# Seven wide steps of a node stage on GpSimd instead of VectorE, in a two-layer graph kernel

## The chip, the cores and the metric

The kernel runs on one core of a Trainium2 chip. A core has a matrix engine (TensorE, PE in the profile), a vector engine (VectorE, DVE), an activation engine (ScalarE, ACT), a general engine (GpSimd, POOL) and a queue engine for transfers (SyncE, SP). Each works through its own queue of instructions in order, and they meet through semaphores. The metric is the device time of one execution in microseconds; the profile's span runs from the first to the last instruction.

## The reference

3327 nodes with 64 features, a dense adjacency matrix of zeros and ones. Two layers, each of the form x = x + layer(relu(layernorm(x))).

```python
# layer 0: hyperbolic attention over neighbours (c = 1 / r^2)
x_t = logmap0(h, c)
left, right = x_t @ w_att[:64, 0], x_t @ w_att[64:, 0]
adj_att = sigmoid(left[:, None] + right[None, :] + b_att[0]) * adj
x_local = logmap(h[:, None, :], h[None, :, :], c)
support = einsum('ij,ijd->id', adj_att, x_local)
out0 = proj(expmap(h, support, c), c)
# layer 1: of each row's neighbours the last 100 count, halved with each step back
rank = cumsum(adj != 0, axis=1); deg = rank[:, -1:]
k = minimum(deg, 100); pos = rank - (deg - k)
w = (adj != 0) * where(pos > 0, 0.5 ** (k - pos), 0)
out1 = w @ (h1 @ weight) + bias
```

Layer 0 needs a value for every pair of nodes. Layer 1 needs, for every pair, how many neighbours lie behind it in its row.

## The kernel before

Nodes are padded to 26 blocks of 128. The pairs are walked in four strips of target nodes, 8, 8, 6 and 4 blocks wide (1024, 1024, 768 and 512 columns), and in each strip over the 26 source blocks from the last to the first. A round is one source block of a strip, except that a round of the last strip takes two, so that all but the third strip's rounds are 1024 columns wide: 91 rounds in all. The main loop runs over the rounds and writes out by hand the order in which PE, DVE and ACT get their instructions.

In a round, PE computes products into a PSUM tile `pq` (lines 680 and 681), counts neighbours into a PSUM tile `pc` from a 0/1 mask (634, 635), and sums finished weights times features into `po` (693). ACT applies two gelus in place to `pq` (873, 874) and a tanh into a tile `sg` (663). DVE does `pair_one`, (sg + 1) * adjacency, both in SBUF (668); `edges`, the mask of a later round from its adjacency tile (623); and `pair_two`, (pq + const) * sg, with `pq` in PSUM (673). The count in `pc` is read out into small integers by `read`, on ACT (652) or on DVE (654, 656); a table `ON_ACT` says for each strip what share of the rounds goes to ACT (1/2, 5/8, 3/4, 1/2).

When a strip ends, its sums `po` are copied out (`strip_out`, 1175 on DVE and 1177 on ACT), transposed by PE (1187, `turn`), copied again (1197, 1199, `per_node`), and then go through `post`, the node stage: norms, the exponential map, the addition to x, layer norm and split of the result into two half-precision parts `s2`, which layer 1 multiplies. For the first three strips this stage is hidden under the next strip's rounds: `post` is a generator, and `advance` takes some of its steps in each round, up to a number of portions. Small steps on 8 or 6 values per partition are collected and given to GpSimd (all at line 1062). Wide steps, on 64 values of each node (512 or 384 per partition), are DVE's: 1080, 1082, 1084, 1140 to 1151, 1156, 1162 and 1167. ACT's wide steps (1154, 1165) wait for a place after the gelus. The last strip's stage is not hidden under rounds; it runs in layer 1, on DVE, among the decoding of weights (1336, 1339, 1340). The bias of layer 1 is added to x by GpSimd (1352). At the end the last four blocks are multiplied (1237), copied (1378 to 1382), multiplied by the weight (1390), added to x (1392) and stored.

The order around a round's stage:

```python
        pair_one(n)
        if two: read(m, js(m)[0])
        if EARLY <= m + 1 < R: edges(m + 1)
        if fresh: count(m, js(m)[-1])
        if n + 1 < R: sigmoids(n + 1)
        if fresh: read(m, js(m)[-1])
        if 4 <= n < R - 1: products(n + 1)
        if ended: strip_out(k - 1)
        if hi - lo > 1: advance(PORTIONS[k])
        pair_two(n)
        advance(PORTIONS[k])
```

Of the kernel before, what the change touches and what calls it, by code (L numbers as in the profile page):

```python
# [12 lines left out]
F32 = mybir.dt.float32  # L13
# [5 lines left out]
AF = mybir.ActivationFunctionType  # L19
ALU = mybir.AluOpType  # L20
# [3 lines left out]
P = 128  # L24
N = 3327
NB = 26
NP = NB * P
D = 64
# [5 lines left out]
AHEAD, LOADS = 1, 4  # L34
EARLY = 3
SGB, ADB = 5, 5
ON_ACT = ((1, 2), (5, 8), (3, 4), (1, 2))


PORTIONS, LAST = (2, 4, 4, 8), 8  # L40
BIG, LATER, ACT = 4, 99, 100
ROUND = (3.5, 3.5, 2.8, 1.9)

LEAD = 7
# [405 lines left out]
def fast(ctx, tc, x, adj_t, r, w_att, b_att, weight, bias, out, flag):  # L450
# [76 lines left out]
    def wide(t, n):  # L527
        return t[:, :, None].to_broadcast([P, n, D])
# [91 lines left out]
    def edges(n):  # L620
        mask_of[n] = mask = work.tile([P, FMAX], BF16, name="mask", bufs=3)
        args = mask[:, : span(n)], ad_of[n][:, : span(n)]
        V.tensor_scalar(*args, 0.0, None, op0=ALU.not_equal)  # L623
# [17 lines left out]
    def read(n, j, on_act=None):  # L641
        k, lo, hi = rounds[n]
        S = strips[k]
        kept = behind(j)[:, S.i0 : S.i0 + S.F]
        num, den = ON_ACT[k]
        i = NB - 1 - j
        of = S.pc[:, : S.F]
        if j in JD:
            kept = by_parity(weight_of[:, j - JD.start])[:, :, S.i0 // 2 : (S.i0 + S.F) // 2]
            of = of.rearrange("p (k r) -> p r k", r=2)  # L650
        if on_act or (on_act is None and i * num // den != (i + 1) * num // den):
            A.activation(kept, of, AF.Relu, scale=128.0 if j in JD else 1.0)  # L652
        elif j in JD:
            V.tensor_scalar(kept, of, 0.0, 128.0, op0=ALU.max, op1=ALU.mult)
        else:
            V.tensor_scalar(kept, S.pc[:, : S.F], 0.0, None, op0=ALU.max)  # L656

    def sigmoids(n):

        S = strips[rounds[n][0]]  # L660
        sg_of[n] = sg = work.tile([P, FMAX], F32, name="sg", bufs=SGB)
        for j in js(n):
# [205 lines left out]
    A.copy(nz[:, high, 0], zf[:, high])  # L868
    V.tensor_copy(nu[:, high, :D], zf[:, high])

    def gelus(n):
        pq = pq_of[n][:, : span(n)]
        A.activation(pq, pq, AF.Gelu, scale=-WG / QS)  # L873
        A.activation(pq, pq, AF.Gelu, scale=WH)  # L874

    def logits(bs, plr=None):

# [132 lines left out]
    def post(agg, k):  # L1010
# [36 lines left out]
        def root(y, v):  # L1047
# [7 lines left out]
            else:  # L1055
                W.scalar_tensor_tensor(rt, v, -0.5, rt, op0=ALU.mult, op1=ALU.mult)
                W.scalar_tensor_tensor(y, rt, 1.5, y, op0=ALU.add, op1=ALU.mult)

        def after(time):

            for do, args, kwargs in asked_of_w:
                do(*args, **kwargs)  # L1062
                if not hidden:
                    yield from [LATER] * 2 if kwargs.get("op") == ALU.pow else [1]
            asked_of_w.clear()
            if hidden:
                yield from [LATER] * math.ceil(time / ROUND[k + 1])

        def both(t):
            return t[:, None, :].to_broadcast([P, 2, nb])  # L1070
# [6 lines left out]
        u, w = tile_of("u", nb, D), tile_of("w", nb, D)  # L1077

        A.activation(u, v, AF.Square)
        V.tensor_mul(w, hs, v)  # L1080
        yield BIG
        V.tensor_reduce(dots[:, 1], w, AX.X, ALU.add)  # L1082
        yield BIG
        V.tensor_reduce(dots[:, 2], u, AX.X, ALU.add)
# [14 lines left out]
        root(rn, t0)  # L1099
        mul(t0, t0, rn)  # L1100
        mul(t0, t0, sk[:, bs])
        yield from after(8.5)
        yield ACT
        A.activation(k_, t0, AF.Tanh)
        yield 0
# [34 lines left out]
        V.tensor_mul(w, hs, wide(of_end[:, 0], nb))  # L1140
        yield BIG
        V.tensor_mul(u, v, wide(of_end[:, 1], nb))
        yield BIG
        V.tensor_add(xs, xs, w)
        yield BIG
        V.tensor_add(xs, xs, u)
        yield BIG

        V.tensor_reduce(t0, xs, AX.X, ALU.add)
        yield BIG  # L1150
        V.scalar_tensor_tensor(w, wide(t0, nb), -1.0 / D, xs, op0=ALU.mult, op1=ALU.add)  # L1151
        yield BIG
        yield ACT
        A.activation(u, w, AF.Square)
        yield 0
# [8 lines left out]
        yield ACT  # L1164
        A.copy(s2[:, bs, 0], w)
        yield 0
        V.tensor_sub(s2[:, bs, 1], w, s2[:, bs, 0])
        yield BIG

    def strip_out(k):  # L1170
        S = strips[k]
        S.ot = work.tile([P, FMAX], F32, name="sg", bufs=SGB)[: D + 1]
        for po, (f0, f1) in zip(S.po, S.hv):
            if f0 == 0:
                V.tensor_copy(S.ot[:, f0:f1], po[: D + 1, : f1 - f0])
            else:
                A.copy(S.ot[:, f0:f1], po[: D + 1, : f1 - f0])
# [23 lines left out]

    class Stage:
        def __init__(self, portions):
            self.portions, self.asked = portions, False

    def advance(portions):
        for stage in stages:
            while portions > 0 and not stage.asked:
                portion = next(stage.portions, LATER)
                stage.asked = portion == ACT  # L1210
                if portion >= LATER:
                    break
                portions -= portion

    def asked_of_act():
        for stage in stages:
            if stage.asked:
                next(stage.portions)
                stage.asked = False

    def finish():
        for stage in stages:
# [21 lines left out]
    for n in range(2, R):  # L1244
# [13 lines left out]
            pa = turn(k - 1)  # L1258
        if n >= 4 and (apart or not turned):
            total(n - 2)  # L1260
        gelus(n)
        asked_of_act()
        if turned and not apart:
            finish()
            stages.append(Stage(per_node(k - 1, pa)))
# [2 lines left out]
            read(m, js(m)[0])  # L1268
        if EARLY <= m + 1 < R:
            edges(m + 1)  # L1270
        if n == 2:
            for j in js(2):
                read(2, j, True)
# [3 lines left out]
            total(1)  # L1277
        if fresh:
            count(m, js(m)[-1])
        if n + 1 < R:  # L1280
            sigmoids(n + 1)
        if fresh:
            read(m, js(m)[-1])
        if 4 <= n < R - 1:
            products(n + 1)
        if ended:
            strip_out(k - 1)
        if hi - lo > 1:
            advance(PORTIONS[k])
        if turned and apart:  # L1290
# [29 lines left out]
        add(j, behind(j), n)  # L1320
    pa = turn(len(STRIPS) - 1)
    pairs.close()
    with tc.tile_pool(name="l1", bufs=2, reuse_waits="tile") as l1, tc.manual_schedule(engines=IN_ORDER):
        decoded = 0

# [21 lines left out]
        for n, j in beside:  # L1347
            add(j, behind(j), n)

        def bias(b0, nb):  # L1350
            xb = x_sb[:, b0 : b0 + nb]
            G.tensor_add(xb, xb, bias_b[:, None, :].to_broadcast([P, nb, D]))  # L1352

        for i, j in enumerate(order):
            for jn in every[: i + 1 + LEAD]:
                if jn not in weights:
                    weights[jn] = decode(jn)
            asked_of_act()
            advance(LAST)
            for n in range(len(chunks)):  # L1360
                if j not in JD or n > 4:
                    add(j, weights[j], n)
            if i % 4 == 3 and i < STRIPS[-2][0]:
                bias(i - 3, 4)
# [93 lines left out]
```

## Time and profile before

| | us |
|---|---|
| three runs | 404.16, 401.86, 404.40 (median 404.16) |
| the profiled execution | 404.32 |
| its span | 402.6 |
| mean granted clock of PE | 0.99 |

The busy time of an engine is what it spent in instructions; a row of a group gives the line, the engine, the operation, output and inputs, the shape, the count, then busy us and mean ns of one, then idle time of the engine just before and what ended it. A row of the timeline gives the start in us, the duration, and in brackets the wait before it and the releaser.

GpSimd's 240 instructions before are almost all small: those of line 1062 on 8 values per partition take from 0.20 us to 2.7 us.

### The profile page before, as it was taken

Reading aid. Unit: us, or ns where it says so; the run is one execution under the profiler, and the core shown is the slowest. Engines: PE = TensorE matmul, PEld = TensorE weight load, DVE = VectorE, ACT = ScalarE, POOL = GpSimd, SP = SyncE. Lnnn points to the kernel's source line nnn. Section 1 sums busy time; section 2 is a strip of 40 time slices with the busy share of each in tenths; the row PEclk is TensorE's granted clock in tenths of the full one; section 3 lists DMA queues with packets and bytes.
Section 4 is the critical chain, followed back from the end, with each engine's and each line's share of the span. In section 5 each row is a group of like instructions: output and inputs, shape, how many; then the busy total and the mean of one; then the engine's idle time right before and its main releaser. Section 6 shows DMA issues by size and latency. Waiting matters only on the chain.

```text
span 402.6 us, 4731 instructions
## 1 busy us (share of the span) xinstructions
PE 355.0 (88%) x1460; PEld 151.9 (38%) x1460; DVE 367.3 (91%) x563; ACT 355.3 (88%) x407; POOL 118.1 (29%) x240
## 2 busy tenths in 40 slices
PE   0087999999999999999999899999979899999992
PEld 0063333333333333333333444444433233344462
DVE  4989999999999989999999999899999999898941
ACT  3589999999999999999999999999998999869510
POOL 8145200000000053870052052850240767241200
PEclk9999999999999899999999999999999999999997
DMA  7314555454548435553445545544563440000012
GB/s 202 150 42 133 171 157 158 128 165 138 163 139 237 148 106 156 156 157 109 153 116 148 149 120 157 131 134 128 152 188 117 111 152 0 0 2 1 2 42 52
DMA packets 23298, 48.99 MB, mean 122 GB/s; under 512 B 8789, under 2 KB 9245, under 8 KB 23265
## 3 DMA queue, kind: packets, MB, share of 16 engines
q1 hardware_dynamic: 20993, 47.66, 40.3%
q10 hardware_dynamic: 1808, 0.46, 0.6%
q0 software_dynamic: 464, 0.49, 0.5%
q8 instruction: 13, 0.21, 0.2%
q14 instruction: 20, 0.16, 0.1%
HBM read 46.40 MB, written 0.87 MB: 117 GB/s over the span
## 4 chain that ended last, share of the span: by engine, by line
DVE 32%; ACT 32%; PE 19%; issue 12%; DMA 1%; POOL 1%; POOLq 0%; DVEq 0%; ACTq 0%
ACT sg L663 11%; ACT pq L873 9%; DVE sg L673 8%; DVE sg L668 7%; PE po L693 7%; ACT behind_lo L652 3%; ACT pq L874 3%; PE pc L635 2%; PE pc L634 2%; PE pq L680 2%; PE pq L681 2%; ACT weight_of L652 2%; DVE behind_hi L656 2%; DVE mask L623 1%; ACT behind_hi L652 1%
## 5 line engine op out<-in xcount | busy, mean ns | idle before, releaser
L693 PE MATMUL po<-sg,hw 128*65 128x512 f32 (+1 forms) x364 | 159.5, 561 | 0.0
L673 DVE SCALAR_TENSOR_TENSOR sg<-pq,sg 128x1024 f32<-128x1024 f32 (+1 forms) x91 | 103.8, 1140 | 4.4 <-ACT pq L874 3.8
L668 DVE SCALAR_TENSOR_TENSOR sg<-sg,ad 128x1024 f32<-128x1024 f32 (+1 forms) x91 | 104.1, 1144 | 0.2
L663 ACT ACTIVATE sg<-left_b,right 128x1024 f32<-128x1024 f32 (+2 forms) x103 | 99.5, 978 | 0.0
L874 ACT ACTIVATE pq<-pq 128x1024 f32<-128x1024 f32 (+1 forms) x91 | 86.2, 947 | 2.9
L873 ACT ACTIVATE pq<-pq 128x1024 f32<-128x1024 f32 (+1 forms) x91 | 87.1, 958 | 1.1 <-PE pq L681 0.9
L693 PEld LDWEIGHTS po<-sg,hw 128*65 128x65 f32 x364 | 49.0, 137 | 67.3 <-issue 53.9
L634 PE MATMUL pc<-mask,ca 128*128 128x512 bf16 (+1 forms) x175 | 64.0, 366 | 10.1 <-ACT behind_hi L652 2.8
L680 PE MATMUL pq<-iu,ju 71*128 71x512 f16 (+1 forms) x182 | 67.5, 371 | 1.6 <-ACT jz L810 1.0
L635 PE MATMUL pc<-mask,cb 128*128 128x512 bf16 (+1 forms) x182 | 65.2, 369 | 1.8 <-ACT behind_lo L652 1.7
L681 PE MATMUL pq<-iz,jz 128*128 128x512 f16 (+1 forms) x182 | 65.9, 369 | 0.0
L623 DVE TENSOR_SCALAR mask<-ad 128x1024 bf16<-128x1024 f32 (+1 forms) x91 | 58.8, 647 | 0.0
L1062 POOL TENSOR_TENSOR dots<-dots,ih 128x8 f32<-128x8 f32 (+1 forms) x3 | 3.1, 1022 | 130.0 <-DVE dots L1082 130.0
L635 PEld LDWEIGHTS <-cb 128*128 128x128 bf16 x182 | 17.8, 98 | 51.8 <-issue 40.3
L634 PEld LDWEIGHTS <-ca 128*128 128x128 bf16 x175 | 17.2, 98 | 29.5 <-issue 17.3
L680 PEld LDWEIGHTS <-ju 71*128 71x128 f16 x182 | 17.9, 99 | 23.1 <-DVE sg L673 5.1
L1237 PEld LDWEIGHTS <-s 128*128 128x128 f16 x182 | 17.7, 98 | 20.2 <-issue 1.5
L681 PEld LDWEIGHTS <-jz 128*128 128x128 f16 x182 | 18.1, 99 | 19.1 <-issue 2.1
L652 ACT ACTIVATE behind_lo<-pc 128x1024 uint8<-128x1024 f32 (+2 forms) x29 | 24.9, 859 | 0.0
L1352 POOL TENSOR_TENSOR x_sb<-x_sb,bias_b 128x256 f32<-128x256 f32 (+1 forms) x6 | 8.6, 1443 | 51.7 <-DVE w L1151 46.0
L652 ACT ACTIVATE behind_hi<-pc 128x1024 uint8<-128x1024 f32 (+2 forms) x25 | 21.8, 871 | 1.2 <-PE pc L635 1.2
L844 PE MATMUL pq<-id,nui 128*71 128x128 f16 x8 | 1.0, 311 | 21.2 <-ACT nzi L818 21.2
(336 smaller groups left out, 396.0 us busy)
## 6 DMA issues: line engine op xcount, KB each, us to landing
ad<-in_adj_t SPq DMA_DIRECT2D x65, 512.0 KB, 3.6
ad<-in_adj_t SPq DMA_DIRECT2D x26, 384.0 KB, 3.1
out<-o SPq DMA_DIRECT2D x6, 128.0 KB, 1.9
left_b<-left_d SPq DMA_DIRECT2D x1, 512.0 KB, 5.0
x_sb<-in_x ACTq DMA_DIRECT2D x1, 416.0 KB, 5.7
x_sb<-in_x SPq DMA_DIRECT2D x1, 416.0 KB
left_b<-left_d SPq DMA_DIRECT2D x1, 384.0 KB
jz<-iz POOLq DMA_DIRECT2D x2, 128.0 KB, 2.6
```

Source lines behind the costliest of these rows:

```text
L623: V.tensor_scalar(*args, 0.0, None, op0=ALU.not_equal)
L634: T.matmul(S.pc[:, f0:f1], ca, S.before[:, f0:f1], start=False, stop=True, skip_group_check=True)
L635: T.matmul(S.pc[:, f0:f1], cb, now[:, f0:f1], start=S.first, stop=True, skip_group_check=True)
L652: A.activation(kept, of, AF.Relu, scale=128.0 if j in JD else 1.0)
L663: A.activation(part(n, sg, j), S.left[:, : S.F], AF.Tanh, bias=right[:, j : j + 1], scale=0.5)
L668: V.scalar_tensor_tensor(sg, sg, 1.0, ad_of.pop(n)[:, :w], op0=ALU.add, op1=ALU.mult)
L673: V.scalar_tensor_tensor(sg, pq_of.pop(n)[:, :w], WD, sg, op0=ALU.add, op1=ALU.mult)
L680: T.matmul(part(n, pq, j, f0, f1), ju[:KB, j, :], S.iu[:, f0:f1], start=True, stop=False)
L681: T.matmul(part(n, pq, j, f0, f1), jz[:, j, :], S.iz[:, f0:f1], start=False, stop=True)
L693: T.matmul(po[: D + 1, : f1 - f0], hw[:, j, :], part(n, sg_of[n], j, f0, f1), start=j == NB - 1, stop=j == 0)
L873: A.activation(pq, pq, AF.Gelu, scale=-WG / QS)
L874: A.activation(pq, pq, AF.Gelu, scale=WH)
```

## The change

Seven wide steps of each hidden stage go from DVE to GpSimd: the product for the first dot, the two products and two additions of the update, the subtraction of the mean (the mean's scaling becomes a small step of its own), and the last subtraction for `s2`. They are given out at a new place in the round, after `edges`, when the last read was ACT's or in the last strip; the four update steps go in two groups of two. Ahead of each step GpSimd copies one column of the newest mask into the step's output, so that the step cannot start before that mask is written. The update's first sum goes to `agg` instead of `x_sb`.

The table `ON_ACT` is gone: reads alternate between ACT and DVE, and the one after a wide step on DVE is ACT's; in the last strip the second read of a round is ACT's. The strip copies come before the tanh and the read. In the last two strips the first tanh of the next round stands between the two gelus. Two bias additions go to DVE near the end. The order of PE's instructions is the same as before.

```diff
-ON_ACT = ((1, 2), (5, 8), (3, 4), (1, 2))
-BIG, LATER, ACT = 4, 99, 100
+BIG, LATER, ACT, POOL = 4, 99, 100, 101
...
     def read(n, j, on_act=None):
+        if hi - lo > 1:
+            on_act = j == lo
...
-        if on_act or (on_act is None and i * num // den != (i + 1) * num // den):
+        if on_act is None:
+            on_act = wide_step[0] or not last_on_act[0]
+            if not wide_step[0]:
+                last_on_act[0] = on_act
+            wide_step[0] = False
+        if on_act:
             A.activation(kept, of, AF.Relu, scale=128.0 if j in JD else 1.0)
...
+    def gelu(n, scale):
+        pq = pq_of[n][:, : span(n)]
+        A.activation(pq, pq, AF.Gelu, scale=scale)
...
+        def on_pool(*steps):
+            if hidden:
+                yield POOL
+                for op, to, *of in steps:
+                    if last_mask[0] is not None:
+                        G.tensor_copy(to[:, 0, :1], last_mask[0][:, :1])
+                    getattr(G, op)(to, *of)
+                yield 0
+            else:
+                for op, *args in steps:
+                    getattr(V, op)(*args)
+                    yield BIG
...
-        V.tensor_mul(w, hs, v)
-        yield BIG
+        if hidden:
+            G.tensor_copy(w[:, 0, :1], last_mask[0][:, :1])
+            G.tensor_mul(w, hs, v)
+            yield LATER
+        else:
+            V.tensor_mul(w, hs, v)
+            yield BIG
...
-        yield from after(8.5)
+        yield from after(7)
...
-        V.tensor_mul(w, hs, wide(of_end[:, 0], nb))
-        yield BIG
-        V.tensor_mul(u, v, wide(of_end[:, 1], nb))
-        yield BIG
-        V.tensor_add(xs, xs, w)
-        yield BIG
-        V.tensor_add(xs, xs, u)
-        yield BIG
+        yield from on_pool(("tensor_mul", w, hs, wide(of_end[:, 0], nb)), ("tensor_mul", u, v, wide(of_end[:, 1], nb)))
+        yield from on_pool(("tensor_add", v, xs, w), ("tensor_add", xs, v, u))
+        if hidden:
+            yield LATER
         V.tensor_reduce(t0, xs, AX.X, ALU.add)
         yield BIG
-        V.scalar_tensor_tensor(w, wide(t0, nb), -1.0 / D, xs, op0=ALU.mult, op1=ALU.add)
-        yield BIG
+        W.tensor_scalar(t0, t0, 1.0 / D, None, op0=ALU.mult)
+        do_asked()
+        yield from on_pool(("tensor_sub", w, xs, wide(t0, nb)))
...
-        V.tensor_sub(s2[:, bs, 1], w, s2[:, bs, 0])
-        yield BIG
+        yield from on_pool(("tensor_sub", s2[:, bs, 1], w, s2[:, bs, 0]))
...
     def advance(portions):
                 portion = next(stage.portions, LATER)
-                stage.asked = portion == ACT
+                wide_step[0] |= portion == BIG
+                stage.asked = portion if portion in (ACT, POOL) else None
...
-        gelus(n)
-        asked_of_act()
+        tanh_first = k > 1 and n + 1 < R
+        gelu(n, -WG / QS)
+        if tanh_first:
+            sigmoids(n + 1, slice(1))
+        gelu(n, WH)
+        list(asked_of(ACT))
...
             edges(m + 1)
+            last_mask[0] = mask_of[m + 1]
+        if last_on_act[0] or k + 1 == len(STRIPS):
+            list(asked_of(POOL))
...
+        if ended:
+            strip_out(k - 1)
         if n + 1 < R:
-            sigmoids(n + 1)
+            sigmoids(n + 1, slice(tanh_first, None))
         if fresh:
             read(m, js(m)[-1])
         if 4 <= n < R - 1:
             products(n + 1)
-        if ended:
-            strip_out(k - 1)
...
         for i, j in enumerate(order):
-            asked_of_act()
+            list(asked_of(ACT))
+            list(asked_of(POOL))
             advance(LAST)
...
-        bias(STRIPS[-2][0], late - STRIPS[-2][0])
-        bias(late, NB - late)
...
             copied(n)
+            if n == 2:
+                bias(STRIPS[-2][0], late - STRIPS[-2][0], V)
+                bias(late, NB - late, V)
```

More of the change, by code (lines that the diff above doesn't have):

```diff
@@ L644, in read @@
         kept = behind(j)[:, S.i0 : S.i0 + S.F]
-        num, den = ON_ACT[k]
-        i = NB - 1 - j
+        if hi - lo > 1:
+            on_act = j == lo
         of = S.pc[:, : S.F]
@@ L656, in read, with sigmoids @@
             V.tensor_scalar(kept, S.pc[:, : S.F], 0.0, None, op0=ALU.max)
-    def sigmoids(n):
+    wide_step, last_on_act, last_mask = [False], [False], [None]
+    def sigmoids(n, of=slice(None)):
         S = strips[rounds[n][0]]
-        sg_of[n] = sg = work.tile([P, FMAX], F32, name="sg", bufs=SGB)
-        for j in js(n):
+        if n not in sg_of:
+            sg_of[n] = work.tile([P, FMAX], F32, name="sg", bufs=SGB)
+        sg = sg_of[n]
+        for j in js(n)[of]:
             A.activation(part(n, sg, j), S.left[:, : S.F], AF.Tanh, bias=right[:, j : j + 1], scale=0.5)
@@ L869, in fast @@
     V.tensor_copy(nu[:, high, :D], zf[:, high])
+    def gelu(n, scale):
+        pq = pq_of[n][:, : span(n)]
+        A.activation(pq, pq, AF.Gelu, scale=scale)
     def gelus(n):
-        pq = pq_of[n][:, : span(n)]
-        A.activation(pq, pq, AF.Gelu, scale=-WG / QS)
-        A.activation(pq, pq, AF.Gelu, scale=WH)
+        gelu(n, -WG / QS)
+        gelu(n, WH)
     def logits(bs, plr=None):
@@ L1057, in root, with do_asked @@
                 W.scalar_tensor_tensor(y, rt, 1.5, y, op0=ALU.add, op1=ALU.mult)
+        def do_asked():
+            for do, args, kwargs in asked_of_w:
+                do(*args, **kwargs)
+            asked_of_w.clear()
         def after(time):
@@ L1203, in __init__ @@
         def __init__(self, portions):
-            self.portions, self.asked = portions, False
+            self.portions, self.asked = portions, None
     def advance(portions):
@@ L1213, in advance, with asked_of @@
                 portions -= portion
-    def asked_of_act():
+    def asked_of(engine):
         for stage in stages:
-            if stage.asked:
+            if stage.asked == engine:
                 next(stage.portions)
-                stage.asked = False
+                stage.asked = None
+                yield engine
     def finish():
@@ L1260, in fast @@
             total(n - 2)
-        gelus(n)
-        asked_of_act()
+        tanh_first = k > 1 and n + 1 < R
+        gelu(n, -WG / QS)
+        if tanh_first:
+            sigmoids(n + 1, slice(1))
+        gelu(n, WH)
+        list(asked_of(ACT))
         if turned and not apart:
@@ L1322, in fast @@
     pairs.close()
+    last_mask[0] = None
     with tc.tile_pool(name="l1", bufs=2, reuse_waits="tile") as l1, tc.manual_schedule(engines=IN_ORDER):
@@ L1348, in fast, with bias @@
             add(j, behind(j), n)
-        def bias(b0, nb):
+        def bias(b0, nb, engine=G):
             xb = x_sb[:, b0 : b0 + nb]
-            G.tensor_add(xb, xb, bias_b[:, None, :].to_broadcast([P, nb, D]))
+            engine.tensor_add(xb, xb, bias_b[:, None, :].to_broadcast([P, nb, D]))
         for i, j in enumerate(order):
```

## The prediction

> **What bounds the kernel now.** I read the busy shares first, then busy time by stretch, then the groups kept apart by shape, then the timeline where engines meet, and last the waits of the tail.
>
> ```profile
> PE 355.0 (88%) x1460; PEld 151.9 (38%) x1460; DVE 367.3 (91%) x563; ACT 355.3 (88%) x407; POOL 118.1 (29%) x240
> ```
>
> Three engines are nearly full and GpSimd (POOL) is idle 71% of the time. An average hides where each binds, so the next view cuts the span where DVE's L673 changes strip: 41.8 to 126.9 us is strip 0, then strips 1, 2 and 3 (columns: length, busy PE, PEld, DVE, ACT, POOL, then clock, DMA share, GB/s).
>
> ```profile
> 126.90:223.10 96.20, 92.33 (x319) 34.95 (x318) 93.00 (x103) 94.21 (x102) 34.23 (x62) 0.98 0.49 142
> 223.10:300.30 77.20, 71.06 (x316) 33.57 (x315) 73.31 (x100) 76.25 (x104) 28.44 (x62) 1.00 0.50 142
> 300.30:350.50 50.20, 46.13 (x160) 17.15 (x159) 49.38 (x65) 48.34 (x65) 23.77 (x52) 1.00 0.28 84
> ```
>
> The stage of strip k runs under the rounds of strip k+1, so these rows are where the change acts. In strip 1 all three engines are within 4 us of full. Strip 2 is ACT's: it lacks 1.0 us, DVE 3.9. Strip 3 is DVE's: it lacks 0.8, ACT 1.9. PE's missing time (3.9, 6.1 and 4.1 us) caps what DVE and ACT relief can win: 14.1 us, since the PE order is the same before and after. Strip 0 is unchanged: its rounds alternate 2.87 and 4.00 us, a mean of 3.44, and PE's own spacing (eight matmuls at 0.215, four at 0.43) is 3.44 as well.
>
> The prices:
>
> ```profile
> L673 DVE SCALAR_TENSOR_TENSOR sg<-pq,sg 128x1024 f32<-128x1024 f32 x65 | 79.1, 1216 | 1.4 <-ACT pq L874 0.8
> L656 DVE TENSOR_SCALAR behind_lo<-pc 128x1024 uint8<-128x1024 f32 x10 | 12.2, 1218 | 0.0
> L656 DVE TENSOR_SCALAR behind_lo<-pc 128x768 uint8<-128x768 f32 x3 | 2.9, 951 | 0.2 <-PE pc L635 0.2
> L1140 DVE TENSOR_TENSOR w<-hw,of_end 128x512 f32<-128x512 f32 x2 | 1.4, 682 | 0.0
> L1140 DVE TENSOR_TENSOR w<-hw,of_end 128x384 f32<-128x384 f32 x1 | 0.5, 549 | 0.0
> ```
>
> Durations of neighbours on DVE overlap by about 0.085 us in the timeline (a 1.22 us instruction starts 1.13 after the one before), so I charge 0.60 for a wide step of 512, 0.47 for 384, 1.14 and 0.87 for a read of 1024 and 768; on ACT 0.92 and 0.72 for such reads.
>
> **The change part by part.**
>
> *Wide steps leave DVE.* Seven per stage: two stages of 512 and one of 384: 14 x 0.60 + 7 x 0.47 = 11.7 us off DVE, 4.2 under strip 1, 4.2 under strip 2, 3.3 under strip 3.
>
> *Reads move to DVE.* By the two instruction orders DVE gains one read in strip 1 and four in strip 2; ACT loses them. DVE +1.1 and +3.5, ACT -0.9 and -2.9. Net on DVE without contention: -3.1, -0.7, -3.3.
>
> *What GpSimd pays and gives back.* It gains 21 wide steps, 19 one-column tie copies and 3 scalings, and loses two bias additions. The nearest row is the bias addition; here it is beside DVE:
>
> ```profile
> 286.50 0.95 DVE L668 SCALAR_TENSOR_TENSOR sg<-sg,ad 128x768 f32<-128x768 f32 x1
> 286.67 2.54 POOL L1352 TENSOR_TENSOR x_sb<-x_sb,bias_b 128x256 f32<-128x256 f32 x2 [18.52 <-DVE w L1151]
> 287.37 0.55 DVE L623 TENSOR_SCALAR mask<-ad 128x768 bf16<-128x768 f32 x1
> 287.84 0.95 DVE L673 SCALAR_TENSOR_TENSOR sg<-pq,sg 128x768 f32<-128x768 f32 x1
> 288.71 1.30 DVE L668 SCALAR_TENSOR_TENSOR sg<-sg,ad 128x768 f32<-128x768 f32 x1
> ```
>
> Two things are to be seen. L668 and the mask ran at full speed while GpSimd had already been issued: GpSimd was kept out until 287.92, then did two 256-wide additions by 289.21, 0.64 each. And the second L668 took 1.30 instead of 0.95: it waited 0.35 for the addition in flight. L673, which takes one operand from PSUM, did not. So a 512-wide step costs about 1.25 us in a clear stretch (an estimate, twice 0.62), a 384 one 0.93; doubling the group's mean of 1.31 per 256 would give 2.6, but that mean contains the waiting. The Trainium skill, "SBUF — State Buffer", section "Who interferes with whom", speaks against the change: a DVE instruction with two SBUF inputs or in a two-port mode and a GpSimd instruction exclude each other for the whole instruction, whoever comes second. Both rows agree with the blocking; they differ in size. By the rule, all 21 steps could land on L668 or the mask: 14 x 1.25 + 7 x 0.93 = 24 us of blocking. By the row the cost is only the overhang, 0.35 us for a pair of 256.
>
> The tie makes a pair start when a mask ends, in a round whose read is DVE's (last strip: any round). From there to the next L668 the clear window is read plus L673: 2.28 us in strip 1, 1.74 in strip 2; in strip 3 L673 alone, 1.14. A pair takes two ties (0.5 with gaps: a copy of 128x8 took 0.19 to 0.21) and two steps: 3.0 us, or 2.4 for 384. Overhang 0.7 a pair in strip 1, 1.25 in strip 2 if the second step has just started (0.4 if DVE gets in first), up to 1.2 in strip 3. I take 0.7, 0.9 and 0.6, two pairs each, and 0.3 a stage for the three single steps, which fit at 1.5 us: 1.7 + 2.1 + 1.5 = 5.3 us on DVE; bounds 1 and 24. DVE then stands at -1.4, +1.4, -1.8.
>
> Behind the ties on GpSimd's queue stand only the stage's own small steps; those who wait are DVE's reductions (L1149, L1082), placed a round later, and ACT's square and cast. A round of 2.8 us or more covers a 3.0 us pair begun at its mask and read after the next round's L673. If that cover goes, a reduction stalls DVE by the rest, under 1 us each.
>
> *Tanh between the gelus, strips 2 and 3.* The second gelu starts 1.04 to 1.05 us after the first at 1024 wide, against 0.92 for an independent successor: 0.13 of dependence a round. Filling it saves 26 x 0.13 = 3.4 us of ACT in strip 2 and 1.6 in strip 3. The cost is that the second gelu, which L673 waits for, ends one tanh (0.93) later; the pq buffer comes round every second round (5.9 us), and gelu, L673, products, gelu, tanh, gelu need 4.4, so 1.5 us cover it. ACT is then at -0.9, -6.3, -1.6.
>
> *Strip copies moved up.* At the end of strip 0:
>
> ```profile
> 130.92 0.68 DVE L1175 COPY sg<-po 65x512 f32<-65x512 f32 x1
> 130.94 0.57 ACT L1177 COPY sg<-po 65x512 f32<-65x512 f32 x1
> 131.65 0.81 PE L1187 MATMUL po<-ident,sg 65*128 65x65 f32 x8 [1.68 <-DVE sg L1175]
> ```
>
> Both copies stood behind one long instruction (DVE's read, ACT's tanh) and PE idled 1.68 us. In front of them they start about 1.1 us earlier. The read is then 0.6 later and PE's next count waits for it, after the transposes: part of the 1.1 returns. What follows the gap:
>
> ```profile
> 129.90:132.10 2.20, 0.52 (x8) 0.45 (x8) 2.20 (x3) 2.20 (x4) 0.00 (x0) 1.00 0.82 222
> 132.10:135.60 3.50, 3.50 (x14) 1.46 (x11) 3.50 (x5) 3.47 (x6) 0.00 (x0) 0.51 0.21 42
> ```
>
> PE ran at half clock for 3.5 us, 1.7 us of lost work, just when it was last on the chain of waits (135.8 to 156). The skill's "TensorE: Matmul & The Clock Gate", "What's actually happening", lets the clock fall only after an idle stretch of a whole window, about 3.4 us; by that rule the 1.68 us gap is not the cause and nothing is won back. By the row the fall follows the gap, and -1.7 is to be had. I take half, 0.85. The other two turns have gaps of 0.88 and 0.2: together -0.5.
>
> *Tail.* DVE's chain reaches the last sub of s, for which PE waits 0.8 us at 382. It loses one 384 sub (-0.47) and the stretching of a decode by the bias addition beside it (1.12 against 0.59: -0.5), gains a scaling (+0.17). But ACT's square of strip 2's deviation now stands behind one more 2.96 us decode: ready at 357.8 instead of 351, while DVE wants it at 356.5: +1.3. Sum +0.5. The two bias additions on DVE (0.82) fall while PE works on chunks; hidden, else +0.8. One left_d load stands one adjacency load later on SP, still a round early: 0.
>
> **Sum.** Strip 1: 1.1 x 0.9 (idle) + 0.85 (clock) + 1.0 (the slower of DVE -1.4 and ACT -0.9) = 2.9. Strip 2: DVE becomes the bound, 73.3 + 1.4 = 74.7 plus the usual waiting of 0.8: 1.7, with the turn 0.3 more. Strip 3: 1.7, the smaller of ACT and DVE, turn 0.2. Tail -0.5. Total 6.3 us off the profiled execution's 404.3 (span 402.6 plus 1.7 around it; the median of the runs is 404.16): 398.0 us.
>
> **The rivals.**
> - *The lock takes it all, slower.* Place: L668 and the mask after each pair. For it: the 1.30 row. Against: L673 and the PSUM reads stay free. It decides from 7.1 us of blocking (11.7 less the 4.6 of reads), 30% of the 24. At 16 us of blocking, two thirds, it is about +9 - 3 (copies, tanh): 410 us.
> - *GpSimd gives way.* DVE starts first each time, steps take 2.6 us, the stage runs late and its reductions stall DVE: gain and stalls cancel but copies and tanh remain, 402.
> - *The overhang is small and stalls vanish.* If blocking is 1 us and the clock does not fall: 4.5 + 4 + 3.3 = 12 us, 392.5, near PE's cap.
> - *PE binds already.* Only the gaps at the turns are won: 401.5.
>
> **How the numbers follow.** A one per cent difference is about what can be told from none here. Forecast (395 to 400.1) 0.55; small overhang 0.19; GpSimd gives way or PE binds (400.1 to 408.2) 0.21; lock 0.05. So faster by over 1% 0.74, within 1% 0.21, slower 0.05. The range 392 to 402.5 leaves out the lock, part of the even cases and a gain beyond PE's cap.
>
> **What would show it.** L668 and L623 with a few instructions of 1.5 to 2.5 us right after GpSimd pairs, in all 4 to 7 us over 1.22 and 0.69; wide GpSimd steps near 1.25; no half clock after the first turn; ACT in strip 2 some 6 us less busy, its bound passing to DVE; L874 starting a tanh after L873. I am wrong if the blocking exceeds 7 us, or if the strip rows shrink by less than 3 us together.

## The result, and the profile after

| | before | after |
|---|---|---|
| median of 22 runs | 404.38 us (401.64 to 405.84) | 401.64 us (399.19 to 403.24) |
| ratio, 95% interval | | 0.9932 (0.9915 to 0.9949) |
| the profiled execution | 404.32 us, span 402.6 | 402.69 us, span 401.0 |

The kernel is 2.7 us faster; 6.3 had been forecast. In the kernel after, line 676 is `pair_one` (668 before), 622 the mask, 681 `pair_two`, 1078 the small steps, 1091 a wide step given to GpSimd, 1095 the same step of the last strip on DVE, 1185 ACT's square (1154), 1187 its reduction (1156), 1376 ACT's and 1379/1380 DVE's decodes, 1269 layer 1's matmuls (1237).

Busy time by stretch, the kernel after: strip 1, strip 2, strip 3 up to the copy of the last sums, and from that copy to the end (length, busy PE, PEld, DVE, ACT, POOL, then clock, DMA share, GB/s):

```profile
128.16:221.90 93.74, 91.05 (x320) 34.72 (x319) 92.65 (x98) 92.94 (x101) 41.05 (x75) 1.00 0.50 147
221.90:296.94 75.04, 71.06 (x317) 33.25 (x316) 74.44 (x98) 72.83 (x101) 41.93 (x77) 1.00 0.51 145
296.94:348.49 51.55, 48.39 (x171) 18.20 (x170) 47.79 (x63) 47.07 (x64) 31.24 (x65) 1.00 0.27 81
348.49:401.00 52.51, 41.82 (x223) 22.76 (x220) 32.93 (x103) 24.28 (x16) 9.19 (x11) 0.90 0.08 19
```

The last two stretches of the kernel before, cut at the same events:

```profile
300.33:353.65 53.32, 49.25 (x174) 18.38 (x173) 51.25 (x70) 48.83 (x66) 23.77 (x52) 1.00 0.27 79
353.65:402.60 48.95, 40.25 (x223) 22.14 (x220) 32.13 (x101) 23.77 (x15) 8.69 (x11) 0.96 0.09 20
```

With strips 1 and 2 of before at 96.17 and 77.24 us (cut at the first `pair_two` of each strip), the changed stretches won 2.43 + 2.20 + 1.77 = 6.4 us. Of this, 1.4 is not the change's: strip 1 of before has half clock in this profile, and the same rounds took 94.77 us in e5 below, which has none there; so 5.0 us are the change's, where 6.0 had been forecast without the clock. The last stretch, where little was changed, lost 3.56, and strip 0, which the change does not touch, lost 1.6: PE ran at half clock from 39 to 42 us there, as it did after the first turn in the profile of before. In strip 2 the bound passed from ACT to DVE (74.44 of 75.04), as forecast.

What happens in the tail is read from the timeline (start, duration, and in brackets the wait before it and its releaser). The kernel before:

```profile
350.50 0.51 ACT L1154 ACTIVATE u<-w 128x384 f32<-128x384 f32 x1
...
355.99 0.54 DVE L1156 TENSOR_REDUCE t<-u 128x6 f32<-128x384 f32 x1
...
356.63 0.30 POOL L1062 TENSOR_SCALAR t<-t 128x6 f32<-128x6 f32 x1 [7.08 <-DVE t L1156]
...
361.33 1.42 POOL L1062 TENSOR_TENSOR rn_last<-t_last,nhalf 128x4 f32<-128x4 f32 x1 [0.52 <-DVE t_last L1062]
...
363.10 0.15 DVE L1062 TENSOR_TENSOR rt_last<-rn_last 128x4 f32<-128x4 f32 x1
...
382.75 1.04 PE L1237 MATMUL po<-weight_of,s 128*128 128x512 bf16 x4 [0.77 <-DVE s L1167]
```

The kernel after:

```profile
344.69 0.83 POOL L1091 TENSOR_TENSOR w<-x_sb,t 128x384 f32<-128x384 f32 x1
...
349.26 2.96 ACT L1376 ACTIVATE wt<-behind_lo 128x3328 uint16<-128x3328 uint8 x1
352.13 0.51 ACT L1185 ACTIVATE u<-w 128x384 f32<-128x384 f32 x1
...
352.66 0.55 DVE L1187 TENSOR_REDUCE t<-u 128x6 f32<-128x384 f32 x1 [0.97 <-ACT u L1185]
...
353.31 0.20 POOL L1078 TENSOR_SCALAR t<-t 128x6 f32<-128x6 f32 x1 [7.78 <-DVE t L1187]
353.59 1.66 POOL L1078 TENSOR_TENSOR rn<-t,nhalf 128x6 f32<-128x6 f32 x1
...
358.22 1.41 POOL L1078 TENSOR_TENSOR rn_last<-t_last,nhalf 128x4 f32<-128x4 f32 x1
359.61 0.91 POOL L1091 TENSOR_TENSOR s<-w,s 128x384 f16<-128x384 f32 x1
...
359.67 0.87 DVE L1078 TENSOR_TENSOR rt_last<-rn_last 128x4 f32<-128x4 f32 x1 [0.93 <-POOL rn_last L1078]
...
379.51 1.04 PE L1269 MATMUL po<-weight_of,s 128*128 128x512 bf16 x4 [2.70 <-DVE s L1095]
380.39 3.57 PE L1269 MATMUL pw<-weight_of,s 128*128 128x512 bf16 x8
```

Three losses stand in a row. The mean of strip 2's stage was given out one turn of the loop later, and so the square of the result stands behind the second decode in ACT's queue. It was not its input that was late (GpSimd had it ready at 345.52, and the decode began at 349.26), but its place in the queue; DVE waited 0.97 us for it. GpSimd's small chain for strip 2 began later (353.31, 4.8 us after the copy of the last sums, against 3.0 before), the last strip's root stood behind it, and DVE waited 0.93 more. Then a DVE step on four values took 0.87 us instead of 0.15, beside GpSimd's wide subtraction. The last `s` came 30.55 us after the copy of the last sums; before it was 28.63. PE, whose own work had not changed, idled 2.70 us for it, and then ran at half clock, as this stretch of the same view shows:

```profile
380.50:383.91 3.41, 3.41 (x11) 1.41 (x8) 0.69 (x1) 0.61 (x1) 0.00 (x0) 0.51 0.00 0
```

GpSimd's hold on DVE is read from the groups kept apart by shape (count, then busy us and mean ns of one). Before:

```profile
L668 DVE SCALAR_TENSOR_TENSOR sg<-sg,ad 128x1024 f32<-128x1024 f32 x65 | 79.1, 1216 | 0.2
L623 DVE TENSOR_SCALAR mask<-ad 128x1024 bf16<-128x1024 f32 x65 | 44.4, 685 | 0.0
L668 DVE SCALAR_TENSOR_TENSOR sg<-sg,ad 128x768 f32<-128x768 f32 x26 | 25.1, 964 | 0.0
L623 DVE TENSOR_SCALAR mask<-ad 128x768 bf16<-128x768 f32 x26 | 14.4, 554 | 0.0
```

After:

```profile
L676 DVE SCALAR_TENSOR_TENSOR sg<-sg,ad 128x1024 f32<-128x1024 f32 x65 | 80.8, 1242 | 0.1
L681 DVE SCALAR_TENSOR_TENSOR sg<-pq,sg 128x1024 f32<-128x1024 f32 x65 | 79.0, 1215 | 2.4 <-ACT pq L881 1.7
L622 DVE TENSOR_SCALAR mask<-ad 128x1024 bf16<-128x1024 f32 x65 | 44.6, 688 | 0.5 <-PE pc L633 0.5
L676 DVE SCALAR_TENSOR_TENSOR sg<-sg,ad 128x768 f32<-128x768 f32 x26 | 26.3, 1012 | 0.0
L622 DVE TENSOR_SCALAR mask<-ad 128x768 bf16<-128x768 f32 x26 | 14.9, 573 | 0.0
```

`pair_one` grew by 26 ns in 65 and 48 ns in 26 instructions, the mask by 3 ns in 65 and 19 in 26: 1.7 + 1.2 + 0.2 + 0.5 = 3.6 us. `pair_two`, which takes one operand from PSUM, is unchanged.

### The profile page after: what moved, and what is told of

Its sections match the earlier page's. It is cut to its first block, busy times and chain, and to the rows that moved or that the text cites. A ratio compares the mean times of both kernels' runs of the same rounds, so it can differ in the third digit from the quotient of the medians.

```text
span 401.0 us, 4773 instructions
## 1 busy us (share of the span) xinstructions
PE 355.7 (89%) x1460; PEld 152.0 (38%) x1460; DVE 365.4 (91%) x550; ACT 349.4 (87%) x402; POOL 145.6 (36%) x281
## 4 chain that ended last, share of the span: by engine, by line
ACT 43%; DVE 21%; issue 15%; PE 15%; POOL 3%; DMA 1%; POOLq 0%; ACTq 0%; DVEq 0%
ACT pq L881 17%; ACT sg L671 14%; DVE sg L681 5%; DVE sg L676 5%; PE po L701 4%; ACT behind_lo L656 3%; ACT behind_hi L656 3%; ACT weight_of L656 1%; PE pc L634 1%; PE pw L1269 1%; PE pc L633 1%; PE pq L689 1%; PE pq L688 1%; DMA x_sb<-in_x 1%; DVE behind_hi L660 1%
## 5 line engine op out<-in xcount | busy, mean ns | idle before, releaser
L676 DVE SCALAR_TENSOR_TENSOR sg<-sg,ad 128x1024 f32<-128x1024 f32 (+1 forms) x91 | 107.1, 1176 | 0.1
L671 ACT ACTIVATE sg<-left_b,right 128x1024 f32<-128x1024 f32 (+2 forms) x103 | 100.9, 979 | 0.0
L656 ACT ACTIVATE behind_hi<-pc 128x1024 uint8<-128x1024 f32 (+2 forms) x24 | 20.9, 872 | 3.7 <-PE pc L634 3.7
L656 ACT ACTIVATE behind_lo<-pc 128x1024 uint8<-128x1024 f32 (+2 forms) x26 | 22.4, 861 | 0.0
L660 DVE TENSOR_SCALAR behind_lo<-pc 128x1024 uint8<-128x1024 f32 (+2 forms) x22 | 22.2, 1011 | 0.1
L660 DVE TENSOR_SCALAR behind_hi<-pc 128x1024 uint8<-128x1024 f32 (+2 forms) x16 | 15.7, 982 | 1.9 <-PE pc L634 1.7
```

What stands on the lines that cost most here:

```text
L676: V.scalar_tensor_tensor(sg, sg, 1.0, ad_of.pop(n)[:, :w], op0=ALU.add, op1=ALU.mult)
```

## The experiments

Theory: the tail, through the late square, ate the gain of the rounds. Rival: GpSimd's blocking in the rounds did, or single parts of the change were worth nothing. Beside medians, the stretches are compared at clock 1.00, where kernels with the same code agree within 0.1 us (strip 1 of the kernel after, and of three experiments that leave it alone: 93.74, 93.75, 93.70, 93.67). A star marks a stretch with a fall of the clock in it. Every kernel's last 4 to 7 us are at half clock too, with PE idle; these carry no star.

| kernel | strip 1 | strip 2 | strip 3 to the copy | copy to end | PE's gap before last s | median us | ratio to before, 95% |
|---|---|---|---|---|---|---|---|
| before | 96.17* | 77.24 | 53.32 | 48.95 | 0.77 | 404.38 | |
| after | 93.74 | 75.04 | 51.55 | 52.51* | 2.70 | 401.64 | 0.9932 (0.9915 to 0.9949) |
| e1 square first | 93.75 | 75.01 | 51.55 | 49.67 | 1.52 | 398.94 | 0.9867 (0.9833 to 0.9901) |
| e2 mean, s on DVE | 93.70 | 75.03 | 51.53 | 50.51 | 2.33 | 400.17 | 0.9904 (0.9869 to 0.9939) |
| e3 copies old | 95.57* | 75.00 | 51.28 | 50.88 | 2.68 | 401.26 | 0.9935 (0.9904 to 0.9966) |
| e4 tanh old | 93.32 | 76.00 | 52.21 | 50.87 | 2.69 | 402.09 | 0.9946 (0.9924 to 0.9969) |
| e5 before, late square | 94.77 | 78.48* | 53.33 | 50.98 | 2.53 | 406.57 | 1.0071 (1.0045 to 1.0098) |
| e6 stage step ahead | 93.66 | 75.02 | 51.55 | 49.99 | 1.87 | 399.29 | 0.9877 (0.9839 to 0.9915) |
| e7 wide steps on DVE | 94.24 | 76.13 | 51.94 | 50.59 | 2.43 | 403.70 | 0.9991 (0.9972 to 1.0011) |
| e8 no tie | 93.97 | 75.30 | 51.70 | 51.07 | 2.69 | 402.12 | 0.9957 (0.9937 to 0.9977) |
| e9 ACT first | 93.66 | 75.03 | 51.54 | 50.22 | 2.05 | 400.42 | 0.9910 (0.9878 to 0.9942) |
| e10 old reads | 94.38 | 76.73 | 51.53 | 52.60* | 2.70 | 403.01 | 0.9977 (0.9960 to 0.9995) |
| e11 tail in order | 93.67 | 75.04 | 51.52 | 48.30 | none listed | 398.20 | 0.9845 (0.9814 to 0.9875) |
| e12 same, copies old | 93.86 | 75.03 | 51.27 | 48.32 | 0.17 | 399.02 | 0.9854 (0.9817 to 0.9891) |

### e1: the square alone ahead of the decode

```diff
         for i, j in enumerate(order):
+            if i == 1:
+                list(asked_of(ACT))
             for jn in every[: i + 1 + LEAD]:
```

> One instruction of ACT moves: the square of strip 2's deviation stands ahead of the second decode instead of behind it. Theory (the tail ate the gain: the square came 3 us late, so GpSimd's small chain for strip 2 came late, so the root of the last strip waited behind it, so PE waited 2.70 us for the last s and then ran 3.4 us at half clock): DVE's reduction at line 1187 no longer waits (0.97 before), the last s comes about 1.9 us earlier, PE's gap before it falls to about 0.8 us, no half clock follows, and the time is 398 to 399.5 us (ratio 0.985 to 0.988). Rival (the blocking of DVE by GpSimd in the rounds ate it, the tail is slack): 401 to 402 us (0.993).

```profile
350.86 0.54 DVE L1187 TENSOR_REDUCE t<-u 128x6 f32<-128x384 f32 x1
...
357.85 0.16 DVE L1078 TENSOR_TENSOR rt_last<-rn_last 128x4 f32<-128x4 f32 x1 [0.93 <-POOL rn_last L1078]
...
377.58 1.04 PE L1269 MATMUL po<-weight_of,s 128*128 128x512 bf16 x4 [1.52 <-DVE s L1095]
```

Timeline of e1. The first wait (0.97) and the stretch of `rt_last` (0.87 to 0.16) are gone, the second wait (0.93) is not: GpSimd's chain for strip 2 still starts 0.8 us later than before. The gap fell by 1.2 of the 1.9 us, the last `s` came 1.2 us earlier (1.9 had been forecast), and the time fell by 2.7 to 398.94. The rows of the rounds did not move. The rival, that the tail is slack, is out; the size of the gap was missed by half. The profile accounts for 1.2 of the 2.7 us. The mean granted clock of the six runs is 0.990 against 0.988, which could make about 0.9 us more (an estimate, 0.0023 of 400 us); that fewer falls are the reason is not shown.

### e5: the same harm alone, put into the kernel before

```diff
-            asked_of_act()
+            if i > 0:
+                asked_of_act()
             advance(LAST)
```

> The kernel before, with the harm of the tail alone: ACT's square of strip 2's deviation stands behind the second decode, as it does after the change; nothing else is moved. Theory (the late square is what costs the tail its time): DVE's reduction waits about 1 us for it, the root of the last strip starts about 2 us later counted from the copy of the last sums, PE's gap before the last s grows from 0.77 to 2.0 to 2.7 us, and the time from 404.3 to 405.5 to 407.4 us. Rival (the tail has slack for it, the loss comes from GpSimd's wide steps there): gap under 1.2 us, time 403.8 to 404.8.

```profile
357.30 0.55 DVE L1156 TENSOR_REDUCE t<-u 128x6 f32<-128x384 f32 x1 [0.96 <-ACT u L1154]
...
364.30 0.16 DVE L1062 TENSOR_TENSOR rt_last<-rn_last 128x4 f32<-128x4 f32 x1 [0.93 <-POOL rn_last L1062]
...
383.98 1.04 PE L1237 MATMUL po<-weight_of,s 128*128 128x512 bf16 x4 [2.53 <-DVE s L1167]
```

Timeline of e5. The two waits of the kernel after are there, 0.96 and 0.93, in a kernel whose wide steps are all DVE's. The stretch from the last copy to the end grew by 2.03 us, and the median rose from 403.66 of that comparison to 406.57. So it is the square's place in ACT's queue that costs this, not GpSimd's work.

### e2, e6, e9, e11: mending the tail

e2 gives strip 2's last two subtractions back to DVE:

```diff
+        if k == 2:
+            V.scalar_tensor_tensor(w, wide(t0, nb), -1.0 / D, xs, op0=ALU.mult, op1=ALU.add)
+            yield BIG
+        else:
+            W.tensor_scalar(t0, t0, 1.0 / D, None, op0=ALU.mult)
+            do_asked()
+            yield from on_pool(("tensor_sub", w, xs, wide(t0, nb)))
...
+        if k == 2:
+            V.tensor_sub(s2[:, bs, 1], w, s2[:, bs, 0])
+            yield BIG
+        else:
+            yield from on_pool(("tensor_sub", s2[:, bs, 1], w, s2[:, bs, 0]))
```

> Strip 2's mean subtraction and its last subtraction go back to DVE, as before the change; all else as after it. Theory (tail): ACT asks for the square a step sooner, GpSimd's queue is clear when the root of the last strip comes, and no GpSimd instruction stretches DVE's small steps there; PE's gap before the last s about 0.8 us, time 398 to 399.5 us. DVE pays 0.47 for the last subtraction, so at most 0.5 us more than with the square alone moved. Rival (rounds): 401 to 402.5 us.

```profile
342.50 0.56 DVE L1182 SCALAR_TENSOR_TENSOR w<-t,x_sb 128x384 f32<-128x384 f32 x1
...
347.46 2.96 ACT L1384 ACTIVATE wt<-behind_lo 128x3328 uint16<-128x3328 uint8 x1
...
350.33 0.51 ACT L1189 ACTIVATE u<-w 128x384 f32<-128x384 f32 x1
```

A miss: both waits remained (0.97 and 0.93). In e2's timeline DVE has the difference ready at 343.06, 4.4 us before the second decode begins, and still the square stands behind that decode: it is asked for one turn too late, whichever engine subtracts the mean. Only the 0.71 us of stretching went, and the last subtraction was paid on DVE.

e6 moves strip 2's stage one step ahead as layer 1 begins:

```diff
+            if i == 0:
+                list(asked_of(POOL))
+                assert next(stages[0].portions) == ACT and next(stages[0].portions) == 0
             list(asked_of(ACT))
```

> The kernel after, with strip 2's stage one step ahead when layer 1 begins: the mean subtraction is given out and the square asked for in the first turn of the loop, so that ACT and DVE have the order of the kernel before there. Theory: the last s comes 28.6 to 28.9 us after the copy of the last sums (28.63 before, 30.55 after, 29.38 with the square alone moved), PE's gap is 0.8 to 1.0 us, no half clock follows, time 398.0 to 398.8 us. Rival (the square alone had all there is; what is left is PE's own work): within 0.3 us of 398.9.

Both waits vanished, and the root of the last strip began 7.68 us after the copy, the very figure of before. But two other waits took part of it back: DVE waited 0.96 us for the last strip's tanh and 0.48 for its square, both behind an ACT decode, and the last subtraction stood behind two decodes of DVE instead of one. Last `s` at 29.72, not 28.6 to 28.9; the median, 399.29, is above the theory's range and 0.1 us above the rival's.

e9 puts everything that the stages ask of ACT ahead of the decodes (with the step of e6 kept):

```diff
         for i, j in enumerate(order):
+            if i > 0:
+                list(asked_of(ACT))
             for jn in every[: i + 1 + LEAD]:
```

> As with the stage one step ahead, and in layer 1 what the stages ask of ACT stands ahead of the decodes (the last strip's tanh and its square no longer wait 0.96 and 0.48 us behind a decode). Theory: DVE's waits between the copy of the last sums and the last s fall from 2.24 to 1.0 to 1.2 us, the last s comes 28.4 to 28.7 us after that copy, PE's gap is under 1.0 us; with neither this gap nor the one at the first turn the clock falls in fewer runs (mean granted clock over the runs 0.990 or more, against 0.988 of the kernels before and after), and the time is 397.5 to 398.7 us. Rival (PE's own work binds the end, the gap only moves): 398.9 to 399.5 us. Rival on the clock (the falls come with no regard to gaps): mean clock 0.987 to 0.989.

A miss: the last `s` came at 29.90, later than in e6. ACT's timeline in e9 shows why:

```profile
371.80 0.42 ACT L1185 ACTIVATE u_last<-w_last 128x256 f32<-128x256 f32 x1 [3.93 <-DVE w_last L1095]
372.12 2.96 ACT L1376 ACTIVATE wt<-behind_hi 128x3328 uint16<-128x3328 uint8 x1
374.99 2.96 ACT L1376 ACTIVATE weight_of<-behind_hi 128x3328 uint16<-128x3328 uint8 x1
377.86 0.39 ACT L1196 CAST s<-w_last 128x256 f16<-128x256 f32 x1
```

The square in front of the decodes made ACT idle 3.93 us. It idles as long in e6, but there one of the two decodes had run before that; here both came behind the square, the last cast stood behind both, and DVE waited 0.78 us for the cast. e11 therefore moves only the tanh, leaves the square behind its decode, and asks for the last cast in the turn of its scaling:

```diff
         for i, j in enumerate(order):
+            if i == 6:
+                list(asked_of(ACT))
...
         V.scalar_tensor_tensor(w, w, 0.0, wide(rn, nb), op0=ALU.max, op1=ALU.mult)
-        yield BIG
+        if hidden:
+            yield BIG
         yield ACT
```

(with the step of e6 kept).

> The kernel after, with strip 2's stage one step ahead, the last strip's tanh alone ahead of a decode (its square stays behind one), and the last cast asked for in the same turn of the loop as the scaling before it. Theory (the tail is DVE's chain: 26.2 us of work plus its waits, and PE has 28.2 us of its own from the same start): DVE's waits fall to 1.5 us, the last s comes 27.9 to 28.6 us after the copy of the last sums (29.38 with the square alone moved), PE's gap is 0.4 to 1.0 us, and the time 397.5 to 398.7 us. Rival (the queues of ACT and DVE hand the wait on once more, as with ACT first): gap 1.5 us or more, 398.9 to 400.4 us.

```profile
357.62 0.22 DVE L1078 SCALAR_TENSOR_TENSOR k_last<-k_last,absr,rn_last 128x4 f32<-128x4 f32 x1 [0.27 <-ACT k_last L1138]
...
374.71 0.42 DVE L1095 TENSOR_TENSOR s<-w_last,s 128x256 f16<-128x256 f32 x1
...
375.19 1.04 PE L1270 MATMUL po<-weight_of,s 128*128 128x512 bf16 x4
```

Timeline of e11. The last `s` starts 28.01 us after the copy and PE takes it up with no wait that the view lists. The stretch to the end is 48.30 us, 0.65 shorter than before the change and 2.6 shorter than after it without a fall of the clock (50.9 in e3 and e4). With 398.20 us, inside the theory's range, it is faster than both kernels.

### e3, e12: the strip copies in their old place

```diff
-        if ended:
-            strip_out(k - 1)
         if n + 1 < R:
             sigmoids(n + 1, slice(tanh_first, None))
...
             products(n + 1)
+        if ended:
+            strip_out(k - 1)
```

> The strip copies stand behind the tanh and the read again; all else as after the change. By the sum on record the move was worth 1.0 us of idle time plus 0.5 at the other turns plus 0.85 of clock: the time rises from 401.6 to 403.1 without a fall of the clock, 404 with one after the first turn, and PE's gap at the first turn is 1.6 to 1.7 us again. Rival (the read that is then late gives the gain back): within 0.5 us of 401.6.

The gap at the first turn was back (1.66 us), and in this profile so was the half clock: strip 1 grew by 1.83 us. Yet the median did not rise, as the rival had it. e12 asked once more, with the tail mended:

> The same, with the strip copies in their old place. Trace rows of other runs put the copies at 0.4 us in strip 1 where no half clock falls. Theory A (the falls of the clock come by chance, with or without the gap of 1.7 us at the first turn): time 0.3 to 0.8 us above the kernel with the tail in order, mean granted clock over the runs the same within 0.001. Theory B (the gap at the first turn brings the fall): 1.3 to 2.0 us above, mean clock lower by 0.002 to 0.004.

Rows of e12's profile, first PE's first turn, then busy time in the 3.5 us behind it:

```profile
131.14 0.71 PE L1218 MATMUL po<-ident,sg 65*128 65x65 f32 x8 [1.67 <-DVE sg L1206]
```

```profile
131.50:135.00 3.50, 3.50 (x18) 1.55 (x17) 3.50 (x5) 3.47 (x5) 0.56 (x2) 1.00 0.24 41
```

The same gap, and full clock. The copies are worth 0.19 us in strip 1 (93.86 against 93.67) and cost 0.25 in strip 3: nothing in sum. The mean granted clock of the two kernels' runs is the same (0.9892 and 0.9895, six runs each), and the medians are 0.8 us apart, the upper end of theory A and within the noise of six runs.

### e4, e7, e8, e10: the other parts of the change, one at a time

```diff
-        tanh_first = k > 1 and n + 1 < R
+        tanh_first = False
```

> Both gelus stand together again in the last two strips, the tanh behind them; all else as after the change. By the sum on record ACT pays 0.13 us a round, 3.4 us in strip 2 and 1.6 in strip 3, but DVE is the bound in both strips by then, so of that only 1 to 1.5 us reach the time: 402.5 to 403.2 us. Rival A (ACT still binds, the tanh is the greater part of what the rounds won): 405 to 406.5 us. Rival B (worth nothing): 401.6.

Strips 1 to 3 grew by 1.2 us together (1.0 in strip 2, 0.7 in strip 3, 0.4 back in strip 1), the median by 0.45, within its noise. The forecast of 1 to 1.5 fits the rows; both rivals are out by the rows.

```diff
                 for op, to, *of in steps:
-                    if last_mask[0] is not None:
-                        G.tensor_copy(to[:, 0, :1], last_mask[0][:, :1])
-                    getattr(G, op)(to, *of)
+                    getattr(V, op)(to, *of)
```

(and the first product likewise).

> The kernel after, with the seven wide steps in their new places but given to DVE, without the tie copies. By the sum on record DVE gets 11.7 us of work and is rid of the 4 to 5 us for which GpSimd keeps it waiting; DVE is the bound in strips 2 and 3: the three strip rows together grow by 6 to 7 us, the time to 406 to 408 us. Rival (the moved steps are worth little, because GpSimd's blocking costs what they save; the reads, copies and tanh made the gain): 401 to 403 us.

```profile
128.00:222.24 94.24, 91.25 (x315) 34.53 (x319) 94.14 (x104) 93.31 (x101) 33.48 (x63) 1.00 0.50 146
222.24:298.37 76.13, 70.08 (x311) 33.10 (x315) 76.10 (x106) 72.84 (x101) 32.99 (x63) 1.00 0.52 144
```

Busy time of e7 in strips 1 and 2. DVE is full to 0.1 us, so it is the bound; but the strips grew by only 2.0 us in sum, not by 6 to 7, and the time by 2.1, not by 4 to 6. DVE's busy time in strips 1 to 3 rose by 1.5, 1.7 and 2.0 us, 5.2 in all: much of the moved work had been paid before as blocking (1.8 us in strip 1 and 2.2 in strip 2, added up over single instructions). And 3.2 of the 5.2 us went into time in which DVE had been idle (1.09, 0.60 and 3.76 us in these strips before, 0.10, 0.03 and 2.13 now). The expectation had forgotten that idle time.

```diff
-                    if last_mask[0] is not None:
+                    if False:
                         G.tensor_copy(to[:, 0, :1], last_mask[0][:, :1])
```

(and the tie of the first product).

> The kernel after, without the one-column copies that tie each wide step of GpSimd to a mask. Theory of the lock: steps now start at any time, so more of them meet a DVE instruction with two inputs in SBUF or a mask; the excess of those two DVE instructions over their usual times grows from 4.2 us in all to 6 to 9, and the time to 402.5 to 405. Rival (the tie only holds the stage back): the excess stays at 4 to 5 us, the stage runs earlier, 400.5 to 401.7 us.

Added up over single instructions, the excess of `pair_one` and mask rose from 4.2 to 6.1 us, and strips 1 to 3 grew by 0.6. The time, 402.12, lies below what the lock expected and above what the rival did. The ties earn their place, by half a microsecond.

```diff
-            on_act = wide_step[0] or not last_on_act[0]
-            if not wide_step[0]:
-                last_on_act[0] = on_act
+            num, den = ((1, 2), (5, 8), (3, 4), (1, 2))[k]
+            i = NB - 1 - j
+            on_act = i * num // den != (i + 1) * num // den
+            last_on_act[0] = on_act
```

> The kernel after, with the reads of the counts shared out by the old table (one in two, 5 in 8, 3 in 4 on ACT) in place of the alternation; all else as after. By the sum on record ACT gets 0.9 us in strip 1 and 2.9 in strip 2 back and DVE loses 1.1 and 3.5: strip 1 changes by less than 0.5 us; strip 2 passes from DVE (74.4 of 75.0 busy) back to ACT (72.8 + 2.9) and grows by 0.7 to 1.5 us; time 402.3 to 403.2 us. Rival (the alternation costs DVE what it gives ACT): within 0.4 us of 401.6 or below.

```profile
221.14:297.87 76.73, 71.34 (x312) 33.30 (x315) 72.33 (x94) 75.62 (x105) 42.07 (x77) 1.00 0.50 143
```

Strip 2 of e10: ACT is the bound again (75.62 of 76.73) with DVE at 72.33. Strips 1 and 2 grew by 0.6 and 1.7 us, each a little more than forecast, and the median by 1.4. DVE was blocked for longer too, 5.7 us by single instructions instead of 4.2, so not all of this is the reads' own.

## Why the prediction was wrong

The time fell into the range (392 to 402.5), but the gain, 0.7%, is less than half of the forecast, and the likeliest case, over 1%, did not come. The mechanism in the rounds was right in the main, and so was the place of the loss; the largest term that failed, and the one whose path was wrong, is the tail's, "ready at 357.8 instead of 351, while DVE wants it at 356.5: +1.3. Sum +0.5". Of the 3.6 us between forecast and median, the tail's chain makes 1.4, strip 1 about 1.0 (0.8 of it the copies), and the clock 1.2 (the 0.85 that was not won, and 0.4 between the rows at full clock and the medians).

- *Tail, the failed step.* It was +1.9 us in the chain instead of +0.5, and with the half clock that can follow, +3.6 in the profiled execution. The prediction saw that the square falls behind a decode, and counted DVE's wait for it, which was 0.97. It did not follow the wait to the queue behind: GpSimd's small chain for strip 2 starts from that reduction, and the last strip's root stands behind that chain (0.93 more). It also credited DVE with 0.97 us of lighter work; DVE's busy time between the copy and the last `s` was 26.41 before and 26.51 after, since the subtraction that went to GpSimd came back as a blocked step on four values. e5 shows that the place of the square alone does as much: +2.0.
- *Clock.* -0.85 was credited for the gap at the first turn. Over the runs nothing was won: mean granted clock 0.988 in 22 runs of before (those beside e1 to e4) and 0.988 in 22 of after. The gap of 1.7 us was followed by half clock in the profiles of before and e3, not in those of e5 and e12. One gap was closed, another (2.70 us in the tail) was opened.
- *Strip 1.* Forecast -2.05 without the clock; measured -1.0 (94.77 in e5, whose rounds are those of before, to 93.74). The 1.0 us for the copies was mis-sized: 0.2 (e12). The gap at the turn did shrink by 1.1 us (1.67 in e12, 0.56 in e11), but the read behind the copies then holds up PE for 0.42 us (e11), and where the rest went is not shown.
- *Strips 2 and 3.* Forecast -2.0 and -1.9; measured -2.2 and -1.8. In strip 2 the path was the forecast one. In strip 3 the number was met by another path, partly by luck: GpSimd's blocking was 0.2 us there, not 1.5, and DVE's busy time fell by 3.5. Up to its last `pair_two` the strip won 2.8 us (49.68 to 46.86). From there to the copy PE is busy throughout, and with more work left to do it took 1.05 us back. (The sum also wrote 1.7 there as the smaller of 1.6 and 1.8; it is 1.6.) First before, then after:

```profile
350.01:353.65 3.64, 3.64 (x17) 1.45 (x16) 2.31 (x10) 1.01 (x2) 0.00 (x0) 1.00 0.00 0
343.80:348.49 4.69, 4.69 (x20) 1.73 (x19) 3.39 (x11) 1.62 (x1) 1.10 (x2) 1.00 0.00 0
```

- *Blocking.* Forecast 5.3 us, measured 3.6 by group means or 4.2 by single instructions (1.8, 2.2 and 0.2 in strips 1 to 3); wide steps of 512 took 1.04 to 1.39 us against the estimate of 1.25. The lock rival is out, and so are those in which GpSimd gives way or PE binds, for the rounds.
- *Tanh and bias.* The tanh between the gelus brought the time that was counted (e4). But ACT in strip 2 is 3.5 us less busy (76.29 to 72.83), not some 6. The two bias additions on DVE, 0.89 us at 384.60, lay beside PE's work, as forecast.
- *The sum.* Without the clock term -5.45 was forecast; strips and tail give -1.0 - 2.2 - 1.8 + 1.9 = -3.1. The runs with the highest granted clock (0.994 or 0.995) agree, as far as three runs can: 402.51 and 402.58 before, 399.19 after.

Taken away one at a time, the reads are worth 2.3 us of the strips' 5.0, the wide steps on GpSimd 2.0, the tanh 1.2 and the copies nothing. They are not independent: the alternation of reads is possible because DVE was relieved. The shorter wait `after(7)` and the two bias additions were not taken away alone.

What stays open is what in full decides whether a gap is followed by half clock (a part of it is below); where the falls lie in runs without a profile cannot be seen. That closing gaps raises the mean clock was not shown: e11, with neither gap, has 0.989.

## What to carry to other kernels

When work is moved off a full engine, follow the moved work's last result to the end of the kernel: a stage that finishes one turn later can cost there a good part of what was won in the middle. Price a late instruction by the queues that start from it, not by the one wait that it causes: here 1 us on DVE became nearly 2 through GpSimd's queue, and 3.6 in a profile in which PE's clock fell as well. Moving an instruction to the front of a queue helps only if its input is ready; otherwise it hands the wait to all that stands behind it (e9).

## What was not expected of the hardware

- Half clock came as one stretch of 3.4 us and not after every gap alike. Gaps of 1.66 to 1.70 us at the first turn were followed by it in two profiles of four, gaps of 2.68 to 2.70 in the tail in two of five. The rule that the prediction took from the Trainium skill ("TensorE: Matmul & The Clock Gate", "What's actually happening": a whole idle window) does not cover these falls; neither does "the fall follows the gap". One fall cost 1.2 to 1.7 us of time.
- The clock records that the traces keep show a part of what decides. In all fourteen profiles each stretch of half clock between two of full clock lasted 3.413 us, and each stretch of full clock was a whole number of times as long (before 262.83 us, 77 times; after 10.24 and 337.92 us, 3 and 99 times). So the changes of the clock lie on a grid of 3.413 us, and its place against the kernel differs from profile to profile. At the first turn, by the ends of PE's matmuls, the two gaps that were followed by a fall lay whole within one step of this grid (1.68 us in before, 1.66 in e3); the other two were cut by a line of the grid (largest piece 1.45 us in e5, 1.15 in e12). In the tail, the two that were followed by a fall had 2.49 (after) and 2.56 us (e10) in one step, the other three at most 1.81. The place on the grid is not all that decides: a gap of 1.73 us in strip 2, whole within one step in both profiles, was followed by a fall in e5 and not in before, and four profiles have a fall at 39 to 42 us, in strip 0.
- A DVE step on four values beside GpSimd's subtraction of 384 took 0.87 us instead of 0.15. The exclusion is not a matter of the DVE instruction's size.
- It goes the other way too: the copy of one column on GpSimd took 0.18 us free and 1.37 at worst.
